# Second attention with one query group in each tick, first roots of the channel mix on GpSimd, and its first two normalizations one and two ticks ahead

## The chip, the core and the metric

The kernel runs on one core of one Trainium2 chip. A core has TensorE (PE: matmuls into PSUM, and the loading of weights, PEld), VectorE (DVE), ScalarE (ACT), GpSimd (POOL) and SyncE (SP), which issues transfers. Each engine runs its own instructions in their order; engines wait for each other by semaphores. The metric is device time in microseconds (us), lower is better. "Span" is the time from the first to the last instruction of one profiled execution.

## What is computed

A block of four layers on x (8 batches of 256 tokens, 256 channels, float32), each added to x after a LayerNorm without gain or bias. The first is an attention with 16 heads of 16 channels to a context, the second a soft mixture of eight experts, the third an attention with 16 heads of 64 to the same context, the fourth a channel mix. The change touches the third and the way into the fourth:

```python
def _layernorm(x, axis=-1, eps=1e-05):
    m = jnp.mean(x, axis=axis, keepdims=True)
    v = jnp.var(x, axis=axis, keepdims=True)
    return (x - m) / jnp.sqrt(v + eps)
# third layer: cross attention, 16 heads of 64
q = (x @ w_q).reshape(B, SQ, 16, 64)
k = (cond @ w_k).reshape(B, SKV, 16, 64)
v = (cond @ w_v).reshape(B, SKV, 16, 64)
attn = jnp.einsum('bqhd,bkhd->bhqk', q, k) * 64 ** -0.5
attn = jax.nn.softmax(attn, axis=-1)
out = jnp.einsum('bhqk,bkhd->bqhd', attn, v).reshape(B, SQ, 1024) @ w_out + b_out
# fourth layer: channel mix
x_prev = concatenate([zeros((B, 1, C)), x[:, :-1, :]], axis=1)
xr = mu_r * x + (1.0 - mu_r) * x_prev
xk = mu_k * x + (1.0 - mu_k) * x_prev
r = jax.nn.sigmoid(xr @ W_r.T)
out = r * (jnp.square(jax.nn.relu(xk @ W_k.T)) @ W_v.T)
```

## The kernel before

x stays in SBUF as `x_sb`, 16 tiles of 128 tokens, two for each batch. The first attention and the mixture take the first 902 us of the profile; the second attention follows till 1306, and the channel mix ends the kernel.

**The second attention** is a pipeline of 36 ticks (`for n in range(len(groups) + 4)`, L1524). A step is a pair of heads of one batch, a group is two steps, a batch is four groups. In tick n five stages of five neighbouring groups run, oldest first:

- stage 3, `values` (L1353): the weighted values `o` of group n - 3, 16 matmuls, and the copy to `ot` on ScalarE;
- one entry of the query projection of batch b = n // 4 + 1, for i = n % 4 (below);
- stage 4, `project`, only for the last step of a batch (i = 3): 32 matmul records `po` (16 products of two passes), added to `x_sb` by VectorE (L1381);
- stage 2, `transposes` (L1339): 16 transposes of the attention weights `ex` on TensorE into `pe`, copied to `et` by VectorE and ScalarE in turn (L1349);
- stage 1, `norm` (L1327): reciprocals `rz` on VectorE, and the scaling of `ex` by them on GpSimd (L1333);
- keys of the next pair of batches (i < 2) or values of the next batch (i >= 2), each ending in one copy on ScalarE and one on VectorE;
- stage 0, `scores` (L1299): 16 matmuls `sc`, the row maxima `nm` on VectorE (L1315), and the exponentials on ScalarE (L1320).

A tick is written tick n from here on; it is counted from one start of `o` to the next. In the last ticks there are no keys, values or queries left.

**The query projection** (`proj1`, L1222) has four entries per batch: for i = 0 `xt_piece`, which normalizes the batch (`normed`, two VectorE operations into one of three buffers `xh`), transposes it on TensorE (`pt_x`, four transposes), copies it to `xT` (one buffer) and adds the output bias to `x_sb` on GpSimd; for i = 1 query group 0, for i = 2 group 1, for i = 3 groups 2 and 3. A query group is 8 matmuls and a copy to `QT` on VectorE. Batch 0's pieces run ahead of the loop, behind its keys and values.

**The channel mix** (`channel_mix`, L1422). `mix` normalizes a batch (`xh_ffn`), transposes it (`pt_xf`), copies it to `yT` and forms the two mixtures; `mixed_keys` and `mixed_values` are its products. The statistics of batches 0 to 3 are taken by `ln_half` in tick 20 (8 pairs of BN_STATS and BN_AGGR, a square root on ScalarE, a reciprocal), those of batches 4 to 6 by `rest_of_stats` in tick 33, those of batch 7 behind the loop. The mixes of batches 0 and 1 stand in ticks 33 and 34.

**What sets the order.** All matmuls and transposes of this stage are pinned in the order in which they are written (`keep_in_program_order`, through `matmul` and `transpose`). Of the other engines' instructions only the pinned ones keep their place behind what was written before them on their engine; the rest are placed by a planner that fills idle time and may pull an instruction ahead as soon as its inputs and its buffer are free. `Ordered` (L87) is a wrapper: while `Ordered.held` is true, what goes through `vec` and `gps` is pinned. PSUM tiles of `pq`, `po`, `pe`, keys, values and `pt` share three buffers (`ps_mm`).

The table of ScalarE's functions is loaded when the function asked for is not in the loaded one (ACT_TABLE_LOAD in the profile).

Of the kernel before, what the change touches and what calls it, by code (L numbers as in the profile page):

```python
# [8 lines left out]
F32 = mybir.dt.float32  # L9
I32 = mybir.dt.int32  # L10
U8 = mybir.dt.uint8
AF = mybir.ActivationFunctionType
ALU = mybir.AluOpType
AX = mybir.AxisListType

P = 128
B, S, D, C = 8, 256, 256, 192
# [6 lines left out]
EPS = 1e-5  # L24
# [39 lines left out]
def kernel(ctx: ExitStack, tc: tile.TileContext, a: dict, out: bass.AP):  # L64
# [63 lines left out]
            a["x"][P * n : P * (n + of), :].rearrange("(t p) d -> p t d", p=P),  # L128
        )

    def ln_half(half, name):

        mv = stat.tile([P, 8, 2], F32, tag="mv", name=f"mv_{name}")
        for i in range(8):
            st = stat.tile([P, 6], F32, tag="bst", bufs=4, name=f"bst_{name}_{i}")
            nc.vector.bn_stats(st, x_sb[:, half * 8 + i, :])
            nc.vector.bn_aggr(mv[:, i, :], st)
        rstd = stat.tile([P, 8], F32, tag="rstd", name=f"rstd_{name}")
        nc.scalar.activation(rstd, mv[:, :, 1], AF.Sqrt, bias=epsb)
        nc.vector.reciprocal(rstd, rstd)  # L140
        return mv, rstd

    def ln_tiles(n, of, name):

        mv = stat.tile([P, 4, 2], F32, tag="mvp", bufs=4, name=f"mvp_{name}")
# [9 lines left out]
    def inverse_root(y, v, name):  # L155


        t = stat.tile([P, 8], F32, tag="nt", bufs=1, name=f"nt_{name}")[:, : v.shape[1]]
        vec.tensor_scalar(t.bitcast(I32), v.bitcast(I32), 1, None, ALU.logical_shift_right)
        vec.tensor_scalar(  # L160
            y.bitcast(I32), t.bitcast(I32), -1.0, float(0x5F3759DF), ALU.mult, ALU.add
        )
        for _ in range(3):
            gps.tensor_tensor(t, y, y, ALU.mult)
            gps.tensor_tensor(t, t, v, ALU.mult)
            gps.tensor_scalar(t, t, -0.5, 1.5, ALU.mult, ALU.add)
            gps.tensor_tensor(y, y, t, ALU.mult)

    def tile_stats(mv, i, n, name):
        st = stat.tile([P, 6], F32, tag="bst", bufs=4, name=f"bst_{name}")  # L170
# [992 lines left out]
    with ExitStack() as l1:  # L1163
# [61 lines left out]
        def proj1(b):  # L1225

            to = {}

            def xt_piece():
                mv, rstd = xat_stats[b // 2]
                pt = transposed(normed(b, mv, rstd, "l1", of=4), f"x1_{b}", transpose)
                to["xT"] = p1.tile([P, 2, S], F32, tag="xT", bufs=1, name=f"xT1_{b}")
                nc.vector.tensor_copy(to["xT"], pt)  # L1235
                for t in range(2):
                    nc.gpsimd.tensor_tensor(
                        x_sb[:, 2 * b + t, :], x_sb[:, 2 * b + t, :], bo, ALU.add
                    )

            def q_piece(t2):
                if t2 == 0:
                    to["QT"] = p1.tile([P, 8, S], F32, tag="QT", bufs=2, name=f"QT1_{b}")
                pq = ps_mm(f"q1_{b}_{t2}").rearrange("p (t n) -> p t n", t=2)
                for i in range(2):
                    t = 2 * t2 + i
                    for c in range(2):
                        matmul(
                            pq[:, i, :],
                            lhsT=wq[:, c, t * P : (t + 1) * P],  # L1250
                            rhs=to["xT"][:, c, :],
                            start=(c == 0),
                            stop=(c == 1),
                        )
                nc.vector.tensor_scalar(
                    to["QT"][:, 2 * t2 : 2 * t2 + 2, :], pq, HD1**-0.5, None, ALU.mult
                )

            def values_of(u):

                if u == 0:
                    to["V"] = p1.tile([P, 2, DA], F32, tag="V", bufs=2, name=f"V1_{b}")
                pv = [ps_mm(f"v1_{b}_{u}_{h}") for h in range(2)]
                t0 = S * b + u * P
                cols = [slice(h * 512, (h + 1) * 512) for h in range(2)]
                for h in range(2):
                    matmul(
                        pv[h],
                        lhsT=ctx0T[:, t0 : t0 + P],
                        rhs=wv[:, 0, cols[h]],  # L1270
                        start=True,
                        stop=False,
                    )

                def halves():
                    for h in range(2):
                        r = slice(64 * h, 64 * h + 64)
                        matmul(
                            pv[h],
                            lhsT=ctx1T[r, t0 : t0 + P],  # L1280
                            rhs=wv[r, 1, cols[h]],
                            start=False,
                            stop=True,
                        )
                    nc.scalar.copy(to["V"][:, u, cols[0]], pv[0])  # L1285
                    nc.vector.tensor_copy(to["V"][:, u, cols[1]], pv[1])

                return halves

            qs = [[xt_piece]] + [[lambda t=t: q_piece(t) for t in ts] for ts in ((0,), (1,), (2, 3))]  # L1290
            return to, qs, [lambda u=u: values_of(u) for u in range(2)]

        def steps1(b, to):

# [99 lines left out]
        def stage(k, n):  # L1394
            for step in groups[n] if 0 <= n < len(groups) else ():
                if k < len(step):
                    step[k]()

        to, qs, vs = projs[0]
        for t2 in range(4):  # L1400
            keys(0, t2)()
        for v in vs:
            v()()
        for pieces in qs:
            for piece in pieces:
                piece()

        ffn_stats = {}  # L1410
        homes = []

        def homes_of_mix():
# [6 lines left out]
            homes.extend(dict(zip(names, rows[5 * k : 5 * k + 5])) for k in range(2))  # L1420

        def channel_mix(b):  # L1422
            def mix():
                st = homes[b % 2]
                yT = yTs[b % 2]
                mv, rstd, of = ffn_stats[b]
                pt = transposed(normed(b, mv, rstd, "ffn", of=of), f"xf_{b}", transpose)
                nc.vector.tensor_copy(yT[:, :, 1 : S + 1], pt)
                for k, n in enumerate(("r", "k")):
                    m = st[n].rearrange("p (c n) -> p c n", c=2)  # L1430
                    for c in range(2):
                        i = 2 * k + c
                        nc.scalar.activation(
                            m[:, c, :], yT[:, c, 1 : S + 1], AF.Copy, scale=mu[:, i : i + 1]
                        )
                        nc.vector.scalar_tensor_tensor(
                            m[:, c, :],
                            yT[:, c, 0:S],
                            omu[:, i : i + 1],
                            m[:, c, :],  # L1440
                            ALU.mult,
                            ALU.add,
                        )
# [58 lines left out]
                        y[:, u, :],  # L1502
                    )

            return mix, mixed_keys, mixed_values


        def rest_of_stats(b, of):
            mv = stat.tile([P, 8, 2], F32, tag="mv", name=f"mv_ffn_{b}")
            rstd = stat.tile([P, 8], F32, tag="rstd", name=f"rstd_ffn_{b}")  # L1510
            for i in range(2 * of):
                st = stat.tile([P, 6], F32, tag="bst", bufs=4, name=f"bst_ffn_{b}_{i}")
                nc.vector.bn_stats(st, x_sb[:, 2 * b + i, :])
                nc.vector.bn_aggr(mv[:, (2 * b + i) % 8, :], st)
            part = slice(2 * b % 8, 2 * b % 8 + 2 * of)
            tc.keep_in_program_order(
                nc.scalar.activation(rstd[:, part], mv[:, part, 1], AF.Sqrt, bias=epsb)
            )
            nc.vector.reciprocal(rstd[:, part], rstd[:, part])
            for k in range(b, b + of):  # L1520
                ffn_stats[k] = mv, rstd, 8

        mixes = [channel_mix(b) for b in range(B)]
        for n in range(len(groups) + 4):  # L1524
            b, i = n // 4 + 1, n % 4
            stage(3, n - 3)
            if b < B:
                for piece in projs[b][1][i]:
                    piece()
            stage(4, n - 4)  # L1530
            stage(2, n - 2)
            stage(1, n - 1)


            if i < 2 and n // 8 < B // 2 - 1:
                keys(n // 8 + 1, n % 8 // 4 * 2 + i)()
            elif i >= 2 and b < B:
                projs[b][2][i - 2]()()
            stage(0, n)
            if n == 20:  # L1540
                mv, rstd = ln_half(0, "ffn_0")
                for k in range(4):
                    ffn_stats[k] = mv, rstd, 8
            if n == 33:
                homes_of_mix()
                mixes[0][0]()
                rest_of_stats(4, 3)
            if n == 34:
                mixes[1][0]()
        rest_of_stats(7, 1)  # L1550
        for k in range(1, B + 2):
            for i in range(3):
                if 0 <= k - i < B and (i, k) != (0, 1):
# [63 lines left out]
```

## Time and profile before

| | us |
|---|---|
| median of three runs | 1354.39 |
| lowest and highest | 1349.74, 1356.31 |
| the profiled execution | 1357.19 |
| its span | 1355.2 |
| ticks 8 to 11 (1011.01 to 1060.72) | 49.71 |
| tick 20 (1160.27 to 1173.85) | 13.58 |
| last `po` starts | 1299.54 |
| first keys of the mix start | 1306.45 |

The profile is taken of one execution. Its page gives the busy time of each engine, the span in 40 slices, the chain of waits that ended last, and the costliest groups of instructions by source line. L103 is the line of the `Ordered` wrapper, so everything that goes through `vec` and `gps` carries it, and the tile's name tells which it is. A line of the timeline has the start, the duration, engine, line, operation, output and inputs with their shape, the number of instructions, and in brackets the idle time before it and what ended it. Busy times of TensorE are of pipelined instructions.

### The profile page before, as it was taken

What the parts mean: (1) busy time and instruction counts of PE and PEld (TensorE: products, weight loads), DVE (VectorE), ACT (ScalarE), POOL (GpSimd) and SP (SyncE); (2) the same over time, 40 slices, a digit from 0 to 9 for tenths busy, and PEclk for the clock granted to TensorE, in tenths of its full rate; (3) what the DMA queues carried; (4) which work ended last, traced back from release to release, by engine and by line L of the source; (5) the groups of instructions that cost most, each with busy time, mean ns of one, the idle gap of its engine ahead of it and who ended that gap; (6) DMA issues with size and microseconds to landing.
All of it is one profiled execution on the core that took longest, in us unless ns stands there. A gap on an engine that the chain in (4) does not pass through costs nothing.

```text
span 1355.2 us, 19107 instructions
## 1 busy us (share of the span) xinstructions
PE 1320.8 (97%) x7520; PEld 957.9 (71%) x7520; DVE 559.3 (41%) x1116; ACT 584.0 (43%) x1409; POOL 243.2 (18%) x273
## 2 busy tenths in 40 slices
PE   8999999799999999999999999999999999999998
PEld 5666655477778877878767888866676667577777
DVE  6677766423330233321333110024544444544555
ACT  1644554544432263522625222213545444544663
POOL 2222401301010000100101000013323322323433
PEclk9999998999999999999999999999999999999999
DMA  7100000033325232332414325350000000000001
GB/s 230 48 2 2 1 1 1 1 99 131 102 97 176 88 107 92 132 132 67 132 67 132 133 86 178 101 151 1 0 1 1 1 0 1 1 1 1 1 8 55
DMA packets 59129, 86.85 MB, mean 64 GB/s; under 512 B 3360, under 2 KB 49056, under 8 KB 59040
## 3 DMA queue, kind: packets, MB, share of 16 engines
q1 hardware_dynamic: 58464, 85.11, 19.1%
q8 instruction: 59, 0.97, 0.3%
q10 hardware_dynamic: 576, 0.52, 0.1%
q14 instruction: 30, 0.25, 0.1%
HBM read 83.53 MB, written 2.10 MB: 63 GB/s over the span
## 4 chain that ended last, share of the span: by engine, by line
PE 89%; ACT 5%; DVE 3%; issue 1%; POOL 1%; ACTq 0%; DVEq 0%; POOLq 0%
PE ph L1066 17%; PE pe L1082 16%; PE sc L74 9%; PE q L74 6%; PE o L74 6%; PE k L74 5%; PE po L74 5%; PE pc L1108 4%; PE v L74 4%; PE pe L77 4%; PE pf L1012 3%; PE ln L930 3%; ACT ex L1320 2%; PE pk L74 1%; PE pr L74 1%; PE pf L74 1%
## 5 line engine op out<-in xcount | busy, mean ns | idle before, releaser
L1074 ACT ACTIVATE ht<-ph,b 128x256 f32<-128x256 f32 x256 | 119.3, 474 | 372.1 <-PE ph L1066 371.7
L1066 PE MATMUL ph<-slots,w 128*128 128x256 f32 x1024 | 266.6, 384 | 1.9 <-ACT ht L1074 1.4
L1082 PE MATMUL pe<-w,ht 128*128 128x256 f32 x1024 | 263.2, 381 | 0.0
L1066 PEld LDWEIGHTS ph<-slots,w 128*128 128x128 f32 x1024 | 182.3, 189 | 55.0 <-ACT ht L1074 22.3
L1082 PEld LDWEIGHTS pe<-w,ht 128*128 128x128 f32 x1024 | 192.1, 190 | 29.9 <-DVE slots L1091 4.2
L1333 POOL TENSOR_TENSOR ex<-ex,rz 128x1024 f32<-128x1024 f32 x64 | 120.1, 1898 | 225.9 <-DVE rz L1331 221.3
L1320 ACT ACTIVATE ex<-sc,nm 128x256 f32<-128x256 f32 x256 | 117.4, 484 | 45.5 <-DVE nm L1315 44.2
L74 PE MATMUL sc<-KT,QT 17*128 17x256 f32 (+1 forms) x1024 | 103.4, 384 | 1.5 <-ACT QT L523 1.5
L579 ACT ACTIVATE ex<-sc 128x512 f32<-128x512 f32 x128 | 75.2, 597 | 64.3 <-PE sc L74 57.5
L990 POOL TENSOR_TENSOR es<-es,zs 128x1024 f32<-128x1024 f32 x12 | 22.7, 1892 | 444.7 <-DVE zs L989 444.7
L103 DVE TENSOR_REDUCE NM<-sc 128x2 f32<-128x512 f32 x128 | 86.6, 689 | 36.0 <-PE sc L74 32.0
L1091 DVE TENSOR_TENSOR slots<-pe,b 128x512 f32<-128x512 f32 x32 | 22.1, 692 | 185.1 <-PE pe L1082 185.1
L74 PE MATMUL q<-xT,wq 128*128 128x256 f32 x384 | 93.0, 389 | 0.9 <-ACT V L1285 0.9
L74 PEld LDWEIGHTS sc<-KT,QT 17*128 17x128 f32 (+1 forms) x1024 | 76.7, 189 | 24.2 <-issue 15.1
L74 PEld LDWEIGHTS q<-xT,wq 128*128 128x128 f32 x384 | 69.8, 190 | 25.3 <-issue 10.6
L1315 DVE TENSOR_REDUCE nm<-sc 128x4 f32<-128x1024 f32 x64 | 75.4, 1220 | 6.4 <-PE sc L74 2.8
L74 PE MATMUL po<-wo,ot 128*128 128x256 f32 x320 | 72.5, 382 | 0.0
L77 PE MATMUL pe<-ident,ex 128*128 128x128 f32 x512 | 69.9, 278 | 0.5 <-DVE xT L1235 0.4
L1349 ACT COPY et<-pe 128x512 f32<-128x512 f32 x64 | 37.1, 608 | 71.7 <-PE pe L77 71.1
L74 PEld LDWEIGHTS po<-wo,ot 128*128 128x128 f32 x320 | 60.1, 190 | 10.9 <-issue 3.2
L77 PEld LDWEIGHTS pe<-ident,ex 128*128 128x128 f32 x512 | 56.2, 140 | 14.0 <-issue 8.0
L74 PE MATMUL o<-et,V 128*64 128x256 f32 x512 | 62.8, 385 | 0.9 <-ACT ot L1368 0.9
(222 smaller groups left out, 1674.2 us busy)
## 6 DMA issues: line engine op xcount, KB each, us to landing
w<-in_w_dram SPq DMA_DIRECT2D x64, 1024.0 KB, 5.6
b<-in_b_dram SPq DMA_DIRECT2D x32, 128.0 KB, 6.7
x_sb<-in_x_dram SPq DMA_DIRECT2D x3, 512.0 KB, 6.4
ctx0T<-in_ctxT_dram SPq DMA_DIRECT2D x4, 256.0 KB, 8.2
ctx1T<-in_ctxT_dram SPq DMA_DIRECT2D x8, 128.0 KB, 7.7
se<-in_slots_dram SPq DMA_DIRECT2D x1, 1024.0 KB, 10.1
wq<-in_wq_dram SPq DMA_DIRECT2D x1, 1024.0 KB, 4.8
wo<-in_wo_dram SPq DMA_DIRECT2D x1, 1024.0 KB, 11.6
```

The source lines that it names most:

```text
L74: tc.keep_in_program_order(nc.tensor.matmul(out, lhsT=lhsT, rhs=rhs, start=start, stop=stop))
L77: tc.keep_in_program_order(nc.tensor.transpose(out, in_, ident))
L103: ins = op(*args, **kwargs)
L579: nc.scalar.activation(ex[:, 2 - 2 * i : 4 - 2 * i, :], sc[1 - i][:, :, 1, :], AF.Exp)
L930: nc.tensor.matmul(pl[:, m * 512 : (m + 1) * 512], lhsT=st["xnT"][:, c, t * P : (t + 1) * P], rhs=snT[:, c, m * 512 : (m + 1) * 512], star ...
L1066: nc.tensor.matmul(ph, lhsT=c_["w1"][:, c, hc * P : (hc + 1) * P], rhs=slots[e][:, c * 256 : (c + 1) * 256], start=(c == 0), stop=(c == 1),)
L1074: nc.scalar.activation(ht, ph, AF.Gelu, bias=b1[:, e, hc : hc + 1])
L1082: nc.tensor.matmul(c_["pe"][:, b, :], lhsT=c_["ht"][hc][:, b * SL : (b + 1) * SL], rhs=c_["w2"][:, hc, :], start=(hc == 0), stop=(hc == HI ...
L1108: nc.tensor.matmul(pc[:, :D], lhsT=CT[:, bl, e, t * P : (t + 1) * P], rhs=eos[e][:, bl, :], start=(e == 0), stop=(e == E - 1),)
L1315: nc.vector.tensor_reduce(nm, sc, AX.X, ALU.max, negate=True)
L1320: nc.scalar.activation(ex[:, i, qb, :], sc[:, i, qb, :], AF.Exp, bias=nm[:, i, qb : qb + 1], accum_out=z[:, i, qb : qb + 1],)
L1333: nc.gpsimd.tensor_tensor(ex, ex, rz.rearrange("p h q -> p (h q)").unsqueeze(2).to_broadcast([P, 4, S]), ALU.mult,)
```

## The change

1. Queries: the four query groups of a batch take the four ticks i = 0 to 3, one each. The normalization moves to a piece of its own at the end of tick i = 2 of the batch before, the transposes, the copy to `xT` and the bias to the end of tick i = 3, ahead of the scores. For batch 0 normalization and transposes stand ahead of its keys and values, and those of batch 1 behind batch 0's queries, ahead of the loop.
2. Statistics of the mix: two tiles of a batch in ticks 4m and 4m + 1, behind the scores, from tick 8 on, BN_STATS pinned (`mix_stats`). `ln_half` is gone.
3. Roots for batches 0 to 3: a first guess on VectorE and three Newton steps on GpSimd, one step in each of ticks 22, 23, 24, pinned (`first_roots`). For batches 4 to 6 the square root on ScalarE stays, now in tick 34 behind the mix of batch 1 (`mix_roots`), and for batch 7 behind the loop.
4. The normalizations of batches 0 and 1 for the mix stand in ticks 31 and 32, pinned; later batches keep theirs in `mix`.

```diff
+            def normed_piece():
+                mv, rstd = xat_stats[b // 2]
+                to["xh"] = normed(b, mv, rstd, "l1", of=4)
+
             def xt_piece():
-                mv, rstd = xat_stats[b // 2]
-                pt = transposed(normed(b, mv, rstd, "l1", of=4), f"x1_{b}", transpose)
+                pt = transposed(to["xh"], f"x1_{b}", transpose)
...
-            qs = [[xt_piece]] + [[lambda t=t: q_piece(t) for t in ts] for ts in ((0,), (1,), (2, 3))]
-            return to, qs, [lambda u=u: values_of(u) for u in range(2)]
+            return (
+                to,
+                [lambda t=t: q_piece(t) for t in range(4)],
+                [lambda u=u: values_of(u) for u in range(2)],
+                normed_piece,
+                xt_piece,
+            )
...
-        to, qs, vs = projs[0]
+        to, qs, vs, normed_piece, xt_piece = projs[0]
+        normed_piece()
+        xt_piece()
         for t2 in range(4):
             keys(0, t2)()
         for v in vs:
             v()()
-        for pieces in qs:
-            for piece in pieces:
-                piece()
+        for piece in qs:
+            piece()
+        projs[1][3]()
+        projs[1][4]()
...
+            def mix_normed():
+                mv, rstd, of = ffn_stats[b]
+                Ordered.held = b < 2
+                xh.append(normed(b, mv, rstd, "ffn", of=of))
+                Ordered.held = False
+
             def mix():
+                if b >= 2:
+                    mix_normed()
...
+        def mix_stats(b, t):
+
+            st = stat.tile([P, 6], F32, tag="bst", bufs=4, name=f"bst_ffn_{b}_{t}")
+            tc.keep_in_program_order(nc.vector.bn_stats(st, x_sb[:, 2 * b + t, :]))
+            nc.vector.bn_aggr(halves[b // 4][0][:, (2 * b + t) % 8, :], st)
...
+        def first_roots(step):
+
+            mv, rstd = halves[0]
+            v, t = first["v"], first["t"]
+            Ordered.held = True
+            if step == 0:
+                vec.tensor_scalar(v, mv[:, :, 1], EPS, None, ALU.add)
+                root_guess(rstd, v, t)
+            root_step(rstd, v, t)
+            Ordered.held = False
+
+        def mix_roots(b, of):
+
+            mv, rstd = halves[b // 4]
             part = slice(2 * b % 8, 2 * b % 8 + 2 * of)
             tc.keep_in_program_order(
                 nc.scalar.activation(rstd[:, part], mv[:, part, 1], AF.Sqrt, bias=epsb)
             )
             nc.vector.reciprocal(rstd[:, part], rstd[:, part])
...
             stage(3, n - 3)
             if b < B:
-                for piece in projs[b][1][i]:
-                    piece()
+                projs[b][1][i]()
...
+            if i == 3 and b + 1 < B:
+                projs[b + 1][4]()
             stage(0, n)
-            if n == 20:
-                mv, rstd = ln_half(0, "ffn_0")
-                for k in range(4):
-                    ffn_stats[k] = mv, rstd, 8
+            if i == 2 and b + 1 < B:
+                projs[b + 1][3]()
+            if n >= 8 and i < 2 and n < 34:
+                mix_stats(n // 4 - 2, i)
+            if 22 <= n < 25:
+                first_roots(n - 22)
+            if n in (31, 32):
+                mixes[n - 31][3]()
             if n == 33:
                 homes_of_mix()
                 mixes[0][0]()
-                rest_of_stats(4, 3)
             if n == 34:
                 mixes[1][0]()
-        rest_of_stats(7, 1)
+                mix_roots(4, 3)
+        for t in range(2):
+            mix_stats(7, t)
+        mix_roots(7, 1)
```

`root_step` is four GpSimd operations on 128 x 8 numbers (t = y y, t = t v, t = 1.5 - 0.5 t, y = y t), `root_guess` two VectorE operations (a shift and a subtraction from a constant on the bits); both are parts of the former `inverse_root`, which the first attention uses still.

More of the change, by code (lines that the diff above doesn't have):

```diff
@@ L129, in load_x @@
         )
[L131 to L141, printed above, removed]
     def ln_tiles(n, of, name):
@@ L158, in inverse_root, with root_guess @@
         t = stat.tile([P, 8], F32, tag="nt", bufs=1, name=f"nt_{name}")[:, : v.shape[1]]
+        root_guess(y, v, t)
+        for _ in range(3):
+            root_step(y, v, t)
+    def root_guess(y, v, t):
         vec.tensor_scalar(t.bitcast(I32), v.bitcast(I32), 1, None, ALU.logical_shift_right)
@@ L162, in inverse_root, with root_step @@
         )
[L163 to L167, printed above, removed]
+    def root_step(y, v, t):
+        gps.tensor_tensor(t, y, y, ALU.mult)
+        gps.tensor_tensor(t, t, v, ALU.mult)
+        gps.tensor_scalar(t, t, -0.5, 1.5, ALU.mult, ALU.add)
+        gps.tensor_tensor(y, y, t, ALU.mult)
     def tile_stats(mv, i, n, name):
@@ L1403 @@
             v()()
-        for pieces in qs:
-            for piece in pieces:
-                piece()
-        ffn_stats = {}
+        for piece in qs:
+            piece()
+        projs[1][3]()
+        projs[1][4]()
         homes = []
@@ L1422, in channel_mix @@
         def channel_mix(b):
+            xh = []
+            def mix_normed():
[3 more added lines that the diff above has]
+                Ordered.held = False
             def mix():
+                if b >= 2:
+                    mix_normed()
                 st = homes[b % 2]
                 yT = yTs[b % 2]
-                mv, rstd, of = ffn_stats[b]
-                pt = transposed(normed(b, mv, rstd, "ffn", of=of), f"xf_{b}", transpose)
+                pt = transposed(xh[0], f"xf_{b}", transpose)
                 nc.vector.tensor_copy(yT[:, :, 1 : S + 1], pt)
@@ L1503, in mixed_values @@
                     )
[L1505 to L1514, printed above, removed]
+            return mix, mixed_keys, mixed_values, mix_normed
+        halves = [
+            (
+                stat.tile([P, 8, 2], F32, tag="mv", name=f"mv_ffn_{k}"),
+                stat.tile([P, 8], F32, tag="rstd", name=f"rstd_ffn_{k}"),
+            )
+            for k in range(2)
+        ]
+        ffn_stats = [(*halves[b // 4], 8) for b in range(B)]
+        def mix_stats(b, t):
+            st = stat.tile([P, 6], F32, tag="bst", bufs=4, name=f"bst_ffn_{b}_{t}")
+            tc.keep_in_program_order(nc.vector.bn_stats(st, x_sb[:, 2 * b + t, :]))
+            nc.vector.bn_aggr(halves[b // 4][0][:, (2 * b + t) % 8, :], st)
+        first = dict(
+            v=stat.tile([P, 8], F32, tag="nv", bufs=1, name="nv_ffn"),
+            t=stat.tile([P, 8], F32, tag="nt", bufs=1, name="nt_ffn"),
+        )
+        def first_roots(step):
[9 more added lines that the diff above has]
+            mv, rstd = halves[b // 4]
             part = slice(2 * b % 8, 2 * b % 8 + 2 * of)
@@ L1519, in rest_of_stats @@
             nc.vector.reciprocal(rstd[:, part], rstd[:, part])
-            for k in range(b, b + of):
-                ffn_stats[k] = mv, rstd, 8
         mixes = [channel_mix(b) for b in range(B)]
@@ L1538 @@
                 projs[b][2][i - 2]()()
+            if i == 3 and b + 1 < B:
+                projs[b + 1][4]()
             stage(0, n)
-            if n == 20:
-                mv, rstd = ln_half(0, "ffn_0")
-                for k in range(4):
-                    ffn_stats[k] = mv, rstd, 8
+            if i == 2 and b + 1 < B:
[6 more added lines that the diff above has]
+                mixes[n - 31][3]()
             if n == 33:
```

## The prediction

> **What bounds the kernel now.** First the page's busy shares and slices:
>
> ```profile
> PE 1320.8 (97%) x7520; PEld 957.9 (71%) x7520; DVE 559.3 (41%) x1116; ACT 584.0 (43%) x1409; POOL 243.2 (18%) x273
> ...
> PE   8999999799999999999999999999999999999998
> ```
>
> TensorE is busy nearly throughout; the others are under half. A change that moves work can only win the time in which TensorE waits. The waits by engine for 945 to 1290 us put five of them in one place, keys behind ScalarE's copy of the transposed weights (4.8 us), and then nothing of that size. So I cut the second attention into its ticks (from one start of the weighted-values matmuls, `o`, to the next) and asked for the busy time in each. After the window come its length and TensorE, weight loads, VectorE, ScalarE and GpSimd busy, then the granted clock:
>
> ```profile
> 949.23:961.30 12.07, 12.07 (x75) 8.29 (x73) 5.87 (x10) 6.00 (x20) 3.74 (x2) 1.00 0.00 0
> 961.30:971.35 10.05, 9.27 (x63) 5.72 (x61) 5.71 (x11) 5.79 (x20) 5.22 (x4) 1.00 0.01 2
> 971.35:981.69 10.34, 10.34 (x67) 6.77 (x65) 5.17 (x9) 6.00 (x20) 3.74 (x2) 1.00 0.00 0
> ...
> 992.03:1011.01 18.98, 18.98 (x107) 14.38 (x105) 7.36 (x15) 5.99 (x20) 3.74 (x2) 1.00 0.00 0
> ...
> 1160.27:1173.85 13.58, 11.18 (x62) 6.14 (x60) 7.34 (x13) 7.08 (x21) 3.79 (x2) 0.87 0.00 1
> 1173.85:1184.20 10.35, 10.35 (x67) 6.77 (x65) 5.19 (x9) 6.00 (x20) 3.74 (x2) 1.00 0.00 0
> 1213.52:1219.95 6.43, 6.43 (x54) 4.65 (x53) 5.02 (x10) 5.21 (x19) 1.42 (x1) 1.00 0.00 1
> 1219.95:1227.72 7.77, 7.77 (x59) 5.74 (x57) 4.49 (x8) 5.41 (x19) 3.84 (x3) 1.00 0.01 2
> ```
>
> These are ticks 3, 4, 5, 7, 20, 21, 24 and 25. Tick 4 has no query group, only the four `pt_x` transposes, and yet takes 10.05 us, almost what tick 5 takes with a query group; TensorE is idle in 0.78 of it. Ticks 8, 12 and 16 measure 10.05 too. Tick 20, of the same make, takes 13.58. The timeline of tick 8 says why:
>
> ```profile
> 1015.20 0.62 ACT L1368 COPY ot<-o 128x512 f32<-128x512 f32 x1
> ...
> 1015.66 1.13 ACT L1349 COPY et<-pe 128x512 f32<-128x512 f32 x2
> ...
> 1016.36 1.98 PE L74 MATMUL k<-ctx0T,wk 128*128 128x512 f32 x4 [0.78 <-ACT et L1349]
> ```
>
> ScalarE goes through 16 `ex` instructions, then `ot`, and comes to `et` some 4.7 us after the tick's first `o` (1011.01). In tick 5 `o` and a query group fill that time; in tick 4 TensorE arrives early and stands. And of tick 20:
>
> ```profile
> 1156.53 1.28 ACT L139 ACT_TABLE_LOAD   x1
> ...
> 1158.40 2.09 DVE L103 TENSOR_SCALAR xh_ffn<-x_sb,mv_ffn,rstd_ffn 128x256 f32<-128x256 f32 x2
> ...
> 1161.01 2.34 DVE L1315 TENSOR_REDUCE nm<-sc 128x4 f32<-128x1024 f32 x2
> 1162.30 1.28 ACT L1320 ACT_TABLE_LOAD   x1 [3.07 <-DVE nm L1315]
> ...
> 1168.37 2.05 PE L74 MATMUL k<-ctx0T,wk 128*128 128x512 f32 x2 [1.72 <-ACT et L1349]
> ```
>
> The square root (with its table) ran at the end of tick 19, its reciprocal set free the first mix normalization, that one stood in front of the row maxima (1.5 us late against tick 8), and then the table of Exp came back. TensorE waited 1.72 us, and the clock fell to 0.87.
>
> **The change, part by part**, in TensorE's time.
>
> (a) Ticks 4m+3, m = 0 to 6, lose the second query group. 16 query matmuls took 3.72, 8 took 1.99: 1.73 less, seven times, -12.1.
>
> (b) The `pt_x` transposes of batches 2 to 7 go from ticks 4m to the end of the ticks before, 3 to 23. 16 such transposes in a row take 2.04, so four 0.51: +3.1.
>
> (c) Ticks 4, 8, 12, 16 get a query group for the transposes and so have the make of tick 5: 10.34 for 10.05, +0.29 four times, +1.2. If the wait of 0.78 stayed beside the group, +3.1 more.
>
> (d) Tick 20 also takes the make of tick 21: 13.58 to 10.35, -3.2. The eight statistics, the root and the early normalization leave it.
>
> (e) Tick 24 takes the make of tick 25: 6.43 to 7.77, +1.3.
>
> (f) Before the loop and in tick 0. Query group 0 of batch 1 comes into tick 0: 1.83 (933.30 to 935.13 for 8 matmuls and the step to the next). It now follows directly on the transposes and the copy to `xT`, which has one buffer and cannot be written before the last queries of batch 0 are through. In the trace these transposes end at 928.70, where keys start at once; the copy runs from 929.07 to 929.75. So TensorE would stand till about 929.85: +1.15. On the other side batch 0's transposes go ahead of keys and values, so the 0.88 idle ahead of the first queries (921.28, after the copy of 920.50) goes. Together +2.1.
>
> Sum of (a) to (f): -12.1 + 3.1 + 1.2 - 3.2 + 1.3 + 2.1 = -7.6.
>
> (g) Statistics: two tiles in each of ticks 4m and 4m+1, as many BN_STATS (0.42) and BN_AGGR (0.18) as before. They stand behind the row maxima; VectorE there has 2.30 us idle before the query copy, so nothing. Without that cover 0.6 in each such tick. What waits behind is the query copy, and `x_sb` was added to a tick before, so the ordered statistics have nothing to wait for.
>
> (h) Roots: three VectorE instructions at 0.17 and 12 on GpSimd, 0.28 from start to start (the first attention's rows), 1.1 in each of ticks 22 to 24. GpSimd multiplies for 3.74 of some 10.3, 7.8 in tick 24, and has room; behind them wait the next tick's multiplications, due 5 us later. Nothing; without the cover 1.1 on a product that the transposes want a tick later. Of the roots of batches 4 to 6, the table load moves behind the mixes of tick 34: keys of the mix start at 1306.45, ScalarE is through with both mixes by 1303.4 even with the load ahead of them. Nothing.
>
> (i) The two ordered normalizations, four operations at 0.40. In tick 31 they come behind the row maxima (end 1289.09), with GpSimd multiplying till 1289.81; in tick 32 behind reciprocals that end at 1292.10, with GpSimd multiplying till 1295.58. The next copy on VectorE is due at 1295.40. If they run at 0.40, nothing. The one long row of this operation, 1.77 against a median of 0.41, lay under such multiplications (1156.27 to 1160.01); twice that is 3.5, and the copy is some 0.3 to 0.6 late. I take +0.2.
>
> The Trainium skill, "SBUF — State Buffer", section "Who interferes with whom", says that a VectorE tensor_scalar in its two-port mode and a GpSimd instruction exclude each other, and the one that issues second waits for the whole of the first. The long row agrees with it; by the rule the sum would have 0.6 here where a plain 0.40 has none, and all early normalizations in the same stage would be open to it.
>
> (k) A tick 4m+3 now ends with transposes, a copy of 0.69 to `xT`, and scores. VectorE copies V (0.69), `xT` (0.69), then takes the maxima, due 0.51 later than now because of the transposes: 0 to 0.1 late. The slack of ScalarE in a tick-5 make is some 0.2. Bounds: 0, and 3.2 (tick 20's excess) for each. I take nothing here.
>
> All in all -7.4. The profiled run took 1357.19 (span 1355.2), so its like would take 1349.8. The median of the three runs shown is 1354.39, 2.8 lower: **1347.0**. What a measurement here can tell from no change is 0.5%, 6.8 us.
>
> **Rivals.**
>
> *The wait stays beside the query group.* Against it: tick 5 has the same ScalarE chain and no wait. For it: `et` in tick 5 starts 0.03 us after `ot`, so ScalarE has no reserve, and ticks 4m carry BN_STATS besides. Five waits of 0.78 are 3.9: -3.5, **1350.9**.
>
> *Tick 20's excess moves and doesn't go*, the change not doing what it says: the planner pulls an unordered normalization (batch 2's needs only the roots of tick 24) into a tick of 7.8 or 5.8 us. Before, the same one ran at 1217.30 and 1218.37 for 0.4 each without a wait. If it costs tick 20's 3.2: -4.2, **1350.2**.
>
> *Slower: VectorE late at every block's edge.* At the six edges (ends of ticks 3 to 23) the `xT` copy is new ahead of the maxima, and where a buffer of the three `xh` has just come free, the planner may put the two operations of a later batch in front too, under GpSimd's multiplications. The maxima, the exponentials, `et` and then keys are late in turn, and an idle TensorE loses clock. Tick 20 is that chain once, for 3.2; six are 19.4: +12.0, **1366.4**. It turns slower than before at 1.2 us an edge and measurably at 2.4. For it: transposes of batches 1 to 4 each free a buffer, and in the trace the next normalization follows within 2 us. Against it: these normalizations took 0.38 to 0.41 each, and the table load of 1.28 that stood in tick 20's path is not in it.
>
> **Chances.** Forecast 0.64 (its own range 1343 to 1350), the wait that stays 0.10, the excess that moves 0.08, slower 0.18. Faster by over 0.5% means under 1347.6: 0.52 from the forecast with its small terms spread to the good side as well (the copy in (f) may end sooner, transposes may hide in the step between matmuls), 0.02 from each of the two middle cases: 0.56. Slower by over 0.5%, above 1361.2: 0.17 of the slower case. Within: 0.27. The three runs lie 6.6 apart, so the range reaches from 1342.5 to 1357.5; what is left out is most of the slower case and a little below.
>
> **What would show it.** Ticks 4, 8, 12, 16 and 20 at 10.3 to 10.4 with no wait of keys for `et`; ticks 7, 11, 15 at 17.7 to 17.8; no table load between the first Exp and the end of the scores; a new idle time of 1.1 ahead of the first query group of tick 0, and none ahead of batch 0's queries; clock 1.00 around 1160. The forecast is wrong if the row maxima start more than 0.3 later against the scores in ticks 7, 11, 15 than in tick 5, if waits of keys for `et` stay, or if the last `po` starts later, against the last scores, than the 14.0 us from 1285.55 to 1299.54.

## The result

| | before | changed |
|---|---|---|
| median of nine runs, us | 1352.06 | 1347.19 |
| lowest and highest, us | 1349.74, 1356.31 | 1344.79, 1350.52 |
| span of the profiled execution, us | 1355.2 | 1346.8 |

The ratio is 0.9953 with a 95% interval of 0.994 to 0.9966: faster by 0.47%, clear of no change, and a hair short of 0.5%. 0.9953 of 1352.06 is 6.4 us less (4.6 to 8.1 by the interval); the medians lie 4.9 apart.

The two profiles lie 8.4 us apart, and not all of it is the change's. The last combining matmuls of the mixture (`pc`), ahead of everything that was edited, started at 888.88 before and at 886.04 after. Ten profiles of this study have that start between 882.08 and 888.88. So from here on I compare the *stage*: from that start to the start of the last output projection `po`. Before it is 1299.54 - 888.88 = 410.66, after 1291.12 - 886.04 = 405.08: **5.58 us less**. Behind the last `po` both take the same, 55.7. The 5.58 lies inside the interval of the whole time.

The windows of the changed kernel by tick, the same view as before (window, length, TensorE, weight loads, VectorE, ScalarE, GpSimd, clock); they are ticks 3, 4, 7, 8, 20, 24, 27 and 33:

```profile
948.07:959.20 11.13, 11.13 (x70) 7.10 (x68) 6.10 (x12) 6.00 (x20) 4.42 (x3) 1.00 0.00 0
959.20:969.55 10.35, 10.35 (x67) 6.78 (x65) 5.40 (x9) 5.90 (x20) 4.58 (x4) 1.00 0.01 2
990.23:1008.27 18.04, 18.04 (x102) 13.18 (x100) 6.80 (x13) 6.00 (x20) 4.42 (x3) 1.00 0.00 0
1008.27:1018.62 10.35, 10.35 (x67) 6.78 (x65) 5.40 (x9) 5.89 (x20) 4.58 (x4) 1.00 0.01 2
1155.48:1165.82 10.34, 10.34 (x66) 6.77 (x64) 5.17 (x9) 6.00 (x20) 3.74 (x2) 1.00 0.01 2
1204.55:1212.32 7.77, 7.77 (x59) 5.73 (x57) 4.49 (x8) 5.41 (x19) 1.44 (x1) 1.00 0.00 1
1230.43:1247.68 17.25, 17.25 (x98) 12.85 (x97) 5.86 (x10) 6.00 (x20) 3.74 (x2) 1.00 0.00 1
1282.89:1288.66 5.77, 4.94 (x36) 3.37 (x36) 5.68 (x9) 2.37 (x6) 3.39 (x2) 1.00 0.00 0
```

Ticks 4, 8 and 20 have TensorE busy from end to end; the 0.78 and the 13.58 of before are gone. What is left of TensorE's waits from 890 to 1340 (who waited for whom, total, times, longest):

```profile
PE q L74 <- DVE xT L1232: 0.9, 1, 0.9
PE v L74 <- ACT et L1351: 0.8, 1, 0.8
PE o L74 <- ACT ot L1370: 0.8, 1, 0.8
PE pe L77 <- DVE et L1351: 0.7, 1, 0.7
```

The first is the new wait ahead of tick 0's query group, the second and third were there before (ticks 2 and 33), the fourth is new, in tick 33.

### The profile page after: what moved, and what is told of

Same layout as the page of the kernel before. It is cut to its first block, busy times and chain, and to the rows that moved or that the text cites. A ratio compares the mean times of both kernels' runs of the same rounds, so it can differ in the third digit from the quotient of the medians.

```text
span 1346.8 us, 19104 instructions
## 1 busy us (share of the span) xinstructions
PE 1316.7 (98%) x7520; PEld 955.1 (71%) x7520; DVE 562.4 (42%) x1118; ACT 582.1 (43%) x1406; POOL 245.1 (18%) x285
## 4 chain that ended last, share of the span: by engine, by line
PE 91%; ACT 4%; DVE 3%; POOL 1%; issue 1%; DMA 1%; ACTq 0%; DVEq 0%; POOLq 0%
PE ph L1060 17%; PE pe L1076 16%; PE sc L74 9%; PE q L74 6%; PE o L74 6%; PE po L74 5%; PE k L74 5%; PE pe L77 4%; PE v L74 4%; PE pc L1102 4%; PE ln L924 3%; PE pf L1006 3%; PE pk L74 1%; PE pr L74 1%; PE pf L74 1%; PE pv L74 1%
```

## The experiments

Ten kernels have profiles: the two above and eight of mine. For each the stage, and where it was timed in rounds beside the kernel before, the ratio:

| kernel | `pc` to last `po` | against before | ratio, 95% |
|---|---|---|---|
| before | 410.66 | | |
| changed | 405.08 | -5.58 | 0.9953 (0.9940 to 0.9966) |
| queries alone | 407.04 | -3.62 | 0.9980 (0.9965 to 0.9994) |
| statistics, roots, normalizations alone | 408.01 | -2.65 | 0.9980 (0.9965 to 0.9995) |
| before, one copy of `et` moved | 404.46 | -6.20 | 0.9957 (0.9937 to 0.9977) |
| changed, normalizations in tick 31 | 404.14 | -6.52 | none (one run) |
| changed, transposes behind the query group | 403.32 | -7.34 | none (one run) |
| changed, two `xT` | 404.21 | -6.45 | none (one run) |
| changed, these three and a copy in tick 2 | 400.61 | -10.05 | 0.9933 (0.9918 to 0.9949) |
| copies for queries | 402.25 | -8.41 | 0.9944 (0.9932 to 0.9957) |

Ticks that no edit touches repeat to 0.02 from profile to profile (but for tick 13, 10.45 in two kernels and 10.34 or 10.35 in the others), so one profile of the stage tells tenths apart; one run of the whole time, with a front that varies by 6.8 us, does not.

### The query groups alone

The kernel before with the first part of the change; `ln_half`, `rest_of_stats` and the mixes stand as they were:

```diff
-                for piece in projs[b][1][i]:
-                    piece()
+                projs[b][1][i]()
...
+            if i == 3 and b + 1 < B:
+                projs[b + 1][4]()
             stage(0, n)
+            if i == 2 and b + 1 < B:
+                projs[b + 1][3]()
             if n == 20:
                 mv, rstd = ln_half(0, "ffn_0")
```

> Only the query groups, their normalization and transposes are moved; the statistics, the square root and the normalizations of the channel mix stay as before. Theory (the query group fills the time until ScalarE is free): ticks 4, 8, 12, 16 take 10.3 to 10.4 us with no wait of keys for et, ticks 7, 11, 15 take 18.0; tick 20 keeps an excess of 2.5 to 3.2 over 10.35; 3.3 us less than before in all (after's 5.6 in the stage, less tick 20's 3.2, plus the 0.9 at the end). Rival (the whole gain comes from the root and the early normalizations leaving tick 20): keys still wait some 0.8 in ticks 4m and the time is that of before within 1 us.

Measured: ticks 4, 8, 12, 16 at 10.34 to 10.35 without a wait, ticks 7, 11, 15 at 18.03 to 18.04, tick 20 at 13.25, 3.62 less in the stage. The theory holds. In tick 20 the group does not help, since that chain is later than ScalarE's ordinary one; the timeline of this kernel there:

```profile
1150.29 2.10 DVE L103 TENSOR_SCALAR xh_ffn<-x_sb,mv_ffn,rstd_ffn 128x256 f32<-128x256 f32 x2
...
1153.51 0.72 DVE L103 TENSOR_SCALAR xh_ffn<-x_sb,mv_ffn,rstd_ffn 128x256 f32<-128x256 f32 x2
1154.15 2.34 DVE L1323 TENSOR_REDUCE nm<-sc 128x4 f32<-128x1024 f32 x2
1155.44 1.28 ACT L1328 ACT_TABLE_LOAD   x1 [4.32 <-DVE nm L1323]
...
1161.50 1.98 PE L74 MATMUL k<-ctx0T,wk 128*128 128x512 f32 x4 [2.64 <-ACT et L1357]
```

Two normalizations of the mix, of two operations each, now go ahead of the maxima, the table of Exp is loaded behind them, and keys stand 2.64. This is the slower rival's chain at one edge: it exists, and it came with the root, not with the queries.

### Statistics, roots and normalizations alone

The changed kernel with the query pieces put back where they were:

```diff
-                projs[b][1][i]()
+                for piece in projs[b][1][i]:
+                    piece()
...
-            if i == 3 and b + 1 < B:
-                projs[b + 1][4]()
             stage(0, n)
-            if i == 2 and b + 1 < B:
-                projs[b + 1][3]()
             if n >= 8 and i < 2 and n < 34:
                 mix_stats(n // 4 - 2, i)
```

> Only the statistics, roots and the two ordered normalizations of the channel mix are moved; queries stay as before. Theory: tick 20 falls from 13.58 to 10.05 like its fellows, which keep their wait of 0.78; no table load before the end of the scores; at the end 0.9 is lost in ticks 31 to 33; some 2.6 us less than before. Rival (all from the root): 5 to 6 us less. Both parts together should give the whole: 3.3 + 2.6 = 5.9.

Measured: tick 20 at 10.04, ticks 4 to 16 at 10.04 with 0.77 of waiting in each, tick 33 at 5.78 instead of 4.83, 2.65 less in the stage, as expected. The two parts add to 6.27 where the whole is 5.58; nearly all of the difference is in tick 20, where each part alone takes something from the same wait (13.58 to 13.25, and 13.58 to 10.04) and both together end at 10.34, for the query group that came in.

### Before, with one copy moved

Is it ScalarE that TensorE waits for in ticks 4m? The kernel before, with the second of four copies of `et` on VectorE for the steps that are transposed in these ticks:

```diff
-                        (nc.scalar.copy if i else nc.vector.tensor_copy)(et[:, i, :, :], pt)
+                        (nc.scalar.copy if i and t != 4 else nc.vector.tensor_copy)(et[:, i, :, :], pt)
```

> The kernel before, with one copy of et in each of ticks 4m (the second of the four) on VectorE instead of ScalarE, nothing else. Theory (TensorE waits there for ScalarE, which comes to et only 4.7 us after the tick's first o): ticks 4, 8, 12, 16 fall from 10.05 to 9.1 to 9.4 without a query group, 0.7 to 0.9 each, 3 to 4 us in all. Rival (the three PSUM buffers or the transposes set the length): 10.0 as before, the wait named VectorE instead.

Measured: ticks 4, 8, 12, 16 at 9.21 to 9.22. Tick 8 of it:

```profile
1007.47 1.87 DVE L1349 COPY et<-pe 128x512 f32<-128x512 f32 x3
...
1008.48 0.62 ACT L1368 COPY ot<-o 128x512 f32<-128x512 f32 x1
1008.80 0.30 PEld L74 LDWEIGHTS k<-ctx0T,wk 128*128 128x128 f32 x2 [0.18 <-DVE et L1349]
1008.81 1.98 PE L74 MATMUL k<-ctx0T,wk 128*128 128x512 f32 x4
1008.96 0.62 ACT L1349 COPY et<-pe 128x512 f32<-128x512 f32 x1
```

Keys start while ScalarE is still on `ot`: nothing that they need comes from it any more. The theory holds, and the expected sum was too low: tick 20 gained as well, 9.63 and then 11.30 in tick 21 where before it was 13.58 and 10.35, another 3.0. Of these 1.3 is waiting: TensorE stood 2.40 in these two ticks before (0.42, 0.26 and 1.72) and 1.12 here (0.42 and 0.70). The rest is clock: before, it was 0.53 for 3.60 us (1168.40 to 1172.00, last section), here it stays at 1.00, and 0.47 of 3.60 is 1.7 (an estimate). So about half of tick 20's excess was slow clock and not waiting. In tick 33 the moved copy loses 0.27 (4.82 to 5.09): TensorE waits 0.66 there for GpSimd's `ex`. One condition in the source took as much from the stage (6.20) as the whole change (5.58).

### The normalizations in tick 31

The changed kernel with both ordered normalizations ahead of the long `po`:

```diff
             stage(3, n - 3)
+            if n == 31:
+                mixes[0][3]()
+                mixes[1][3]()
...
-            if n in (31, 32):
-                mixes[n - 31][3]()
```

> The changed kernel with both ordered normalizations set into tick 31 behind the weighted values, ahead of the 7 us of po, where VectorE was idle for 7.5 us. Theory (in tick 32 they stand between two copies of et and run only between GpSimd's multiplications): the wait of 0.74 in tick 33 goes and the last po starts 14.0 to 14.2 after the last scores instead of 14.9. Rival (the pinned statistics or the order in itself cost it): 14.7 to 15.0 as now.

Measured: tick 33 at 4.82, last `po` 13.97 behind the last scores (1287.02 - 1273.05), the fourth wait gone. In the changed kernel VectorE and GpSimd had stood like this; the second ordered normalization is written in tick 32 and falls, by the count from `o` to `o`, into tick 33, which starts at 1282.89 (timeline; the first line has four operations merged, the others are of shorter windows, two of the four and the second of GpSimd's two multiplications by themselves):

```profile
1283.18 3.90 DVE L103 TENSOR_SCALAR xh_ffn<-x_sb,mv_ffn,rstd_ffn 128x256 f32<-128x256 f32 x4
...
1283.18 1.35 DVE L103 TENSOR_SCALAR xh_ffn<-x_sb,mv_ffn,rstd_ffn 128x256 f32<-128x256 f32 x1
...
1284.34 1.94 POOL L1335 TENSOR_TENSOR ex<-ex,rz 128x1024 f32<-128x1024 f32 x1
...
1284.45 1.98 DVE L103 TENSOR_SCALAR xh_ffn<-x_sb,mv_ffn,rstd_ffn 128x256 f32<-128x256 f32 x1
...
1287.00 0.68 DVE L1351 COPY et<-pe 128x512 f32<-128x512 f32 x1
```

GpSimd goes from its first multiplication to its second at 1284.34, and the first operation ends at 1284.53; the second multiplication ends at 1286.28, the second operation at 1286.43. Each operation, 0.40 alone, ends 0.15 to 0.2 behind the multiplication that was running when it was issued. Two unordered ones of batch 2 follow in the 0.65 that remain till 1287.08, and only then, at 1287.00, comes the copy of `et`, whose four transposes had ended at 1286.00. In tick 31 GpSimd multiplies till 1264.31 and then rests for 9 us, and this group of the moved kernel has

```profile
L103 DVE TENSOR_SCALAR xh_ffn<-x_sb,mv_ffn,rstd_ffn x8: 382/400/901, 1263.6 to 1285.7; 128x256 f32<-128x256 f32 x8
```

(shortest, median, longest in ns): a median of 400 for the 670 and a longest of 901, the one that began (1263.55) under GpSimd's last multiplication, for the 1979 that the changed kernel has in 1276 to 1289. The edit takes the ordered normalizations away and batch 2's from behind them at once; no run moves one without the other.

### The transposes behind the query group

```diff
                 projs[b][1][i]()
+            if i == 3 and b + 1 < B:
+                projs[b + 1][4]()
...
-            if i == 3 and b + 1 < B:
-                projs[b + 1][4]()
             stage(0, n)
```

> The changed kernel with the transposes of the next batch and their copy moved within tick 4m+3, from between values and scores to right behind the query group. Theory (the transposes cost 0.79 there instead of the 0.51 that they take in a row, because they stand between the half-height values and scores): ticks 7, 11, 15, 19, 23 fall from 18.04 to 17.7 to 17.8, 1.5 to 1.8 us in all six. Rival (four transposes between other matmuls cost 0.8 wherever they stand): 18.0.

Measured: ticks 7, 11, 15, 19, 23 at 17.69 to 17.70, and 1.76 less in the stage. Tick 3, the sixth, gained only 0.05 (11.13 to 11.08): no `po` stands behind the queries there, and the 16 transposes of `ex` that follow directly took 2.50 instead of 2.20, a weight load of theirs waiting for ScalarE's copy of `et`. Tick 27 has no such transposes and takes 17.25, so they cost 0.44 here and 0.79 in the changed kernel. The weight loads of the changed kernel's tick 7 show where the 0.35 goes:

```profile
1004.70 0.30 PEld L74 LDWEIGHTS v<-wv,ctx1T 64*128 64x128 f32 x4 [0.76 <-issue]
1005.76 0.42 PEld L77 LDWEIGHTS pt_x<-ident,xh_l 128*128 128x128 f32 x4 [0.76 <-issue]
1006.34 1.60 PEld L74 LDWEIGHTS sc<-KT,QT 64*128 64x128 f32 x16 [0.17 <-issue]
```

Without the transposes, in the kernel before, the first scores' weights were loaded 0.24 behind those of the half-height values:

```profile
1008.22 0.30 PEld L74 LDWEIGHTS v<-wv,ctx1T 64*128 64x128 f32 x4 [0.76 <-issue]
1008.76 0.19 PEld L74 LDWEIGHTS sc<-KT,QT 64*128 64x128 f32 x2 [0.23 <-issue]
```

The full-height weight load does not get in beside the half-height values here: it starts with its own matmul, 0.76 later. Behind the queries, which are of full height themselves, the moved kernel loads it without such a gap, 0.21 ahead of its first matmul (989.92):

```profile
989.71 0.58 PEld L77 LDWEIGHTS pt_x<-ident,xh_l 128*128 128x128 f32 x4
```

### Two xT

Batch 1's transposes ahead of batch 0's queries, and a second buffer for the copy:

```diff
-                to["xT"] = p1.tile([P, 2, S], F32, tag="xT", bufs=1, name=f"xT1_{b}")
+                to["xT"] = p1.tile([P, 2, S], F32, tag="xT", bufs=2, name=f"xT1_{b}")
...
+        projs[1][3]()
+        projs[1][4]()
         for piece in qs:
             piece()
-        projs[1][3]()
-        projs[1][4]()
```

> The changed kernel with two buffers for xT and batch 1's transposes ahead of batch 0's queries. Theory (the wait of 0.94 ahead of tick 0's query group is the copy to the one xT): that wait is gone, from the start of the last combining matmuls to the first o 61.0 to 61.2 us instead of 62.03. Rival (the wait turns to the copy of the queries or the PSUM buffers): 61.7 to 62.1.

Measured: from `pc` to the first `o` 61.12 (886.31 to 947.43) against 62.03, the wait of 0.94 gone. Its one whole time was 1347.96 with a late start of the stage; that says nothing against it.

### All three, and a version without the groups

The three edits, and for batch 0's first step `et` as in the experiment with the moved copy (`i and not (b == 0 and t == 0)`):

> The changed kernel with the three edits (normalizations of the mix in tick 31, transposes behind the query group, two xT) and, for the first step of batch 0 alone, the second copy of et on VectorE. Theory: the edits add up, 0.9 + 1.7 + 0.9 and 0.8 for the wait of 0.77 in tick 2: 4.3 us less than the changed kernel in the stage from the last combining to the last po (405.1 to 400.8), some 10 us less than before in all, a ratio of 0.992 to 0.993. Rival (ScalarE and VectorE have no reserve, so some of it turns into new waits): 402.5 to 404.

Measured: 400.61, the sum to within 0.2. All that TensorE still waits for from 890 to 1340:

```profile
PE o L74 <- ACT ot L1370: 0.9, 1, 0.9
```

The ratio, 0.9933, is 0.0003 above the range I gave for it: 9.1 us below before, and below the changed kernel's 0.9953, with intervals that overlap. It is the best of the ten by the stage.

The other way to the same end leaves the queries where they were (`i and not (t == 4 or (b == 0 and t == 0))`, statistics and roots as changed, normalizations in tick 31):

> Queries as before (no group in ticks 4m); statistics and roots of the channel mix as changed, its two normalizations in tick 31, and one copy of et on VectorE in ticks 4m and tick 2. Theory (a lighter ScalarE does for ticks 4m what the query group does): ticks 4, 8, 12, 16 and 20 at 9.2, 402.2 from the last combining to the last po against 405.1 changed and 410.7 before, 8 to 9 us less than before, a ratio of 0.993 to 0.994. Rival (VectorE, with three copies and the statistics, takes over as the one waited for in ticks 4m): 9.6 or more there, 404.

Measured: ticks 4m at 9.21 to 9.22, tick 20 among them, 402.25: as expected, VectorE takes the third copy and the statistics without being waited for in these ticks. In tick 33 TensorE waits 0.66 for GpSimd, as with the moved copy alone (5.09 for 4.82). It stays 1.6 above the other version, of which 0.9 is the wait ahead of batch 0's queries, still there (0.88).

## Why the prediction was right, and where not

The forecast was 1347.0 and the time is 1347.19, but that nearness is part luck: the median of before went from 1354.39 (three runs) to 1352.06 (nine), which took from the starting point about what the gain fell short by; 25 runs of the same kernel beside the experiments have their median at 1354.02. The gain in the stage was 5.58 against 7.6 summed and 7.4 taken. By the steps:

- (a) Exact. Tick 27, which only loses a group, went from 18.98 to 17.25, 1.73.
- (b) **Mis-sized.** Six sets of transposes cost 0.79 each and not 0.51, 1.7 more in all. I took the price in a row of transposes; between half-height matmuls the weight loads lose their overlap. So ticks 7, 11 and 15 came to 18.04, outside the 17.7 to 17.8 that I had named. This is the larger part of what was missing.
- (c), (d), (e) Right to 0.01: 10.34 to 10.35, 10.34, 7.77. That tick 5's length would carry over was the main claim; the moved copy shows the reason, ScalarE's chain, by a second way.
- (f) 1.68 (62.03 less 60.35) for 2.1: the wait for `xT` is 0.94 and not 1.15, and batch 0's transposes, now ahead of full-height keys, take 0.43 (898.99 to 899.42) where behind half-height values they took 0.65 (919.75 to 921.28, less the 0.88 of waiting). It is the same price of height as in (b), here on the good side.
- (g), (h) Nothing, as said: no tick shows them.
- (i) **Mis-sized**: 0.94 for 0.2 (tick 33: 4.83 to 5.77). I had the bound from the 1.77 row, a copy 0.3 to 0.6 late, and took nearly nothing of it; and I missed that batch 2's unordered pair would follow at once. The copy came 1.0 late (1287.00 for 1286.00), and the pair held VectorE for 0.65 of that. So some 0.3 of the 0.94 would be left without the pair, an estimate from these rows. The rule of the Trainium skill that I set beside it ("SBUF — State Buffer", "Who interferes with whom") says why the ordered pair took so long: the operation that issues second waits for the whole of the first; the two ends, 0.15 to 0.2 behind a multiplication's end, agree.
- (k) The planner did put both operations of a later batch's normalization ahead of the maxima, in ticks 3, 7 and 11 (0.73 in tick 7). The maxima start 1.40 behind the first scores there (1006.35 to 1007.75) and 1.08 in tick 5: 0.32 later, in tick 15 0.10. Against the next `o` they start 0.52 ahead instead of 0.75, 0.23 late, and no wait came of it: tick 8 is 10.35.

Of the three signs of being wrong that I had set, two came, then: the maxima more than 0.3 later in ticks 7 and 11, which cost nothing, so that the mark was badly chosen; and the last `po` 14.93 behind the last scores instead of 14.0, which is what (i) had too small. No wait of keys for `et` stayed.

Of the rivals: the wait that stays beside the group has no case in any tick. The excess that moves: tick 20's is gone, and what came up in tick 33 is 0.94, and batch 2's unordered normalization, the one that this rival names, has its part in it, some 0.65 where the rival had put 3.2. Slower at the edges: the chain is real in tick 20 of the queries alone, but six edges without a root cost nothing. Its last link, that an idle TensorE loses clock, did not hold there: 2.64 of waiting, and the clock at 1.00. I gave 0.56 to faster by over 0.5%; it came out at 0.47%, which is the neighbouring box.

The part ahead of the stage varies by 6.8 us between profiles, and no edit touches it. All of that arises in the first 440 us: from the first `pc` to the last combining matmuls the ten profiles take 449.57 to 449.64. Some of it goes with the clock: from the sixth to the seventh `po` of the first attention the five profiles with a clock of 0.68 to 0.92 in 220 to 230 us (0.68 before, 0.82 changed) take 27.8 to 29.5, the five with 1.00 take 26.1 to 26.2. Why the clock falls there in some executions and not in others stays open.

## What to carry to other kernels

When an engine bound at 97% still waits, cut its pipeline into ticks and compare ticks of different make: the one with less work and the same length names the late engine. Then weigh two cures, work to fill the wait and work taken off the late engine; the second was one copy here and as good as the first. A moved piece is to be priced beside its new neighbours, not in a row of its own kind, and an operation that excludes another engine belongs where that engine is idle.

## What was not expected of the hardware

The clock fell in tick 20 of the kernel before and not in tick 20 of the queries alone, though TensorE's longest wait is 1.72 in the first and 2.64 in the second. Windows of the kernel before:

```profile
1165.00:1168.40 3.40, 1.42 (x6) 0.35 (x4) 1.18 (x4) 3.40 (x14) 2.45 (x2) 1.00 0.02 5
1168.40:1172.00 3.60, 3.60 (x6) 1.29 (x8) 0.00 (x0) 0.41 (x1) 1.34 (x1) 0.53 0.00 0
```

and of the queries alone:

```profile
1160.00:1165.00 5.00, 3.50 (x14) 1.75 (x16) 0.56 (x2) 2.36 (x7) 3.02 (x2) 1.00 0.00 0
```

From the end of `o` (1162.15) to 1168.37 the first had only transposes, 1.13 us of keys and waits, 6.2 us. The second had a query group in between, and behind it 4.7 us of transposes and waiting (1156.82 to 1161.50). The Trainium skill, "TensorE: Matmul & The Clock Gate", "Part 4: PE-mode transpose", says that transposes do not count as activity for the gate as matmuls do. No run here shows it by itself: the first stretch agrees with it, but the 4.7 us of the second had no matmul of another kind either, and the clock held. The length of the stretch may be what differs.
